# Gate sums begun by ScalarE's zeros, and a new order of products, in a graph layer with a GRU

## The chip, the cores and the metric

The kernel runs on one core of one Trainium2 chip. The metric is the time on the device in microseconds, the median of several runs. Engines are named as in the profile: PE is TensorE's matrix multiply, PEld its weight load, DVE is VectorE, ACT is ScalarE, POOL is GpSimd, SP is SyncE. Everything is computed in float32.

## The reference

There are 64 graphs of 256 nodes with 256 features, and one 256 x 256 adjacency matrix for each. Cut to what matters:

```python
h = relu(layernorm(x))                                   # (64, 256, 256)
c = relu(bn1(conv1d(h.T, conv1_w, 1 tap)))
x_conv = relu(bn2(conv1d(c, conv2_w, 17 taps)) + h.T).T
s = h @ w_se.T + b_se                                    # 3 columns
A = exp(-squared_distance(s, s)) * adj
x_nmp = A @ relu(h @ w_msg.T + b_msg)
gi = concat([x_conv, x_nmp]) @ w_ih.T + b_ih             # r, z, n
gh = h @ w_hh.T + b_hh                                   # r, z, n
r = sigmoid(gi_r + gh_r); z = sigmoid(gi_z + gh_z)
n = tanh(gi_n + r * gh_n)
out = x + (1 - z) * n + z * h
```

## The kernel before

**Tiling.** Two graphs make a pair `i` (512 columns, since nodes lie on the free axis and 128 features on the partitions), and four pairs make a block `b`. There are 32 pairs in 8 blocks. The loop over blocks is unrolled, and what it emits for one block is one long list in which pairs of this block and preparations of the next (`nxt = i + 4`) are woven by hand. Every engine works through its own instructions in the order in which they were emitted; SP and POOL issue the DMAs likewise.

**A block.** The 17-tap convolution is done for the whole block in a transformed domain. `forward` puts the FFT steps `odd` and `even` for VectorE in a queue, `products(b, 0)` to `products(b, 7)` multiply by the transformed filters (line 767, filters `wb` by DMA), and `branch_back`, `odd_back`, `q_back`, `p_back` and `join` bring the result back into `Yv`. `residual` (line 800) adds the input, and a Relu on ScalarE follows (line 801). Each pair also needs `message` (line 804: four groups of products, additions on VectorE at line 813, and the small tile `z`, lines 816 to 822, on ScalarE), `embed` (line 827: three transposes of `z` and a copy to `zT`, line 831), `affinity` (line 834: four small products at line 841, `exp` at line 842, a multiplication by the adjacency on VectorE at line 848) and `aggregate` (line 863, into `xnm`). `conv1` (line 688) is the one-tap convolution for a pair of the next block; `split_steps` are the first FFT steps on its result. `finish` (line 1107) transposes the output, adds `x`, stores it from POOL's queue and loads the next `y` there.

**Gates.** The first pair of each block gets its gate r from ordinary products on 512 columns (`gates_first`). The other gates, n and z of each pair and r of pairs 1 to 3, are 11 in a block and 88 in all. They use a scheme with seven products for a 2 x 2 split (features by graphs): `combine` builds differences of the inputs on VectorE (lines 906 and 911), `weight_sums` those of the weights, and class `Gate` (line 925) makes the seven products, numbered 1 to 7. A gate has two PSUM banks. Products 1 and 2 share one half of the first bank, 7 and 4 the other; 5 has a half of the second, 6 and 3 share the last. Each product is two (gate n) or three (r, z) full products on 256 columns, which follow each other in the sum. Between them the running sum is copied by ScalarE from half 1 into half 6 (line 949), and from half 6 into half 7 (line 952). Sums are finished in `c11`, `c12`, `c22` and `c21`, with additions on VectorE (lines 984, 998, 1014) and tanh on ScalarE (lines 969, 1021). `gate_hn` (line 1030) and `times_r` (line 1036) make r * gh_n. The order of a pair is `gates_r`, then `gates_nz`, to which the loop hands functions (`between`, `middle`, `last`) with the work to be put in between.

**PSUM.** There are eight banks: a ring of three `aux` and a ring of five `acc` (lines 535 and 538). In the kernel before, a product that begins a half carries the start flag, and a product of zeros on the other half of the bank follows it (line 945).

**Pacing.** The order on VectorE is planned while the program is built: class `Pace` keeps a planned time for TensorE and VectorE, and `pace.vector(n, ready, slack)` first emits as many queued FFT steps as fit before the next operation is `ready`. `pace.flush(mark)` emits all up to a mark. `BULK` is a queue of ScalarE copies (adjacency and inputs, lines 435, 660 and 684), of which each product of a gate emits one.

Of the kernel before, what the change touches and what calls it, by code (L numbers as in the profile page):

```python
# [15 lines left out]
BF = mybir.dt.bfloat16  # L16
# [289 lines left out]
def kernel(  # L306
# [145 lines left out]
    zero = const.tile([1, N], BF, name="zero")  # L452
# [87 lines left out]

    PSUM, ACT = 0.2, 0.9
# [146 lines left out]
    def conv1(i):  # L688
        if i >= B // G:
            return  # L690
        for o in range(DC):
            p = acc()
# [9 lines left out]
        pace.vector(0, pace.pe + ACT)  # L702
# [95 lines left out]
    def residual(i, o):  # L798
        v = xcv(i % PB, o)
        nc.vector.scalar_tensor_tensor(v, v, s2[:, o:o + 1], HT[i][:, o, :], op0=ALU.mult, op1=ALU.add)  # L800
        nc.scalar.activation(v, v, AF.Relu, bias=h2_shift[:, o:o + 1])  # L801


    def message(i):
        MSG[i] = work.tile([P, G, MC, D + SE], FP, name="msg")
        for g in range(G):
            for c in range(MC):
                p = acc() if g * MC + c == 3 else aux()
                for k in range(DC):
                    mm(p[:, :D + SE], chunk(HT[i][:, k], g, c), w_msg[:, k, :], D + SE,  # L810
                       start=(k == 0), stop=(k == DC - 1))
                pace.vector(D, pace.pe + PSUM)
                nc.vector.tensor_add(MSG[i][:, g, c, :], p[:, :D + SE], b_msg)  # L813
# [20 lines left out]
    def affinity(i, early=False):  # L834
        E[i] = work.tile([P, G, MC, N], FP, name="e")
        for g in range(G):
            for c in range(MC):
                q = g * MC + c
                p = acc() if q == 3 and not early else aux()
# [43 lines left out]
    def combine(i, q):  # L883
# [7 lines left out]
        def first():  # L891
# [14 lines left out]
            nc.vector.tensor_sub(TERMS[i, q][0], b(0, 1), b(0, 0))  # L906

# [11 lines left out]
    SOON = -0.4  # L919
# [4 lines left out]

    class Gate:
        def __init__(self, i, gate):
            self.i, self.gate, self.bank = i, gate, [acc(), acc()]

        def half(self, j, other=False):
            n, h = WHERE[j]  # L930
            return graph(self.bank[n], 1 - h if other else h)

        def products(self, *js):
            for j in js:
                out = self.half(j)
                qs = (1, 2) if self.gate == N_ else (0, 1, 2)
                for q in qs:
# [3 lines left out]
                    mm(out, weight(q, self.gate, j), v, N, start=(j in (1, 5) and q == qs[0]), stop=(q == qs[-1]),  # L941
                       skip_group_check=True)
                if j in (1, 5):

                    nc.tensor.matmul(self.half(j, True), zero[:, :P], zero, start=False, stop=True,  # L945
                                     skip_group_check=True)
                    pace.tensor(N / 4)
                if j == 5:
                    nc.scalar.copy(self.half(6), self.half(1))  # L949
# [7 lines left out]
                elif j == 7:  # L957
                    self.c22(out)
                elif j == 4:
                    self.c21(out)  # L960
                if BULK:
                    BULK.popleft()()
# [67 lines left out]
    def gate_hn(i, o):  # L1030
        p = acc()
# [7 lines left out]
    def gates_first(i, early, wait):  # L1039

        p = []
        for o in range(DC):
            gate_hn(i, o)
# [6 lines left out]
        for o in range(DC):  # L1050
            product(p[o], i, (2,), o * P, first=False)
        for steps in zip(*(combine(i, q) for q in (1, 2, 0))):
            run(steps)
        for o in range(DC):
            nc.scalar.activation(tr[:, o], p[o], AF.Tanh, bias=b_rz[:, o:o + 1], scale=0.5)
            times_r(o)

    def gates_r(i, between):
        r = Sigmoid(i, R)
        r.products(1, 5, 2, 6)  # L1060
        between()
        gate_hn(i, 0)
        r.products(3, 7)
        gate_hn(i, 1)
        times_r(0)
        r.products(4)
        times_r(1)

    def gates_nz(i, between, middle, last):
        n = New(i, N_)  # L1070
        if i % PB:
            n.products(1, 5)
            z = Sigmoid(i, Z_)
            z.products(1)
            between()
            n.products(2, 6)
            z.products(5)
# [3 lines left out]
        else:  # L1081
            n.products(1)
            z = Sigmoid(i, Z_)
# [11 lines left out]
        last()  # L1095
# [5 lines left out]
        for o in range(DC):  # L1101
# [3 lines left out]
            nc.vector.scalar_tensor_tensor(d[:, o], d[:, o], 0.5, nn[:, o], op0=ALU.mult, op1=ALU.add)  # L1105

# [114 lines left out]
    message(0)  # L1221
    pace.flush(odd)
    run(fft.sums(V, Sv, 0, 0))
    for b in range(NB):
        i = b * PB
        nxt = i + PB
        if b > 0:
            affinity(i)
            load_adj(i + 1)
# [4 lines left out]
        if b > 0:  # L1234
            finish(i - 1)
        else:
            embed(i)
        products(b, 1)
        pace.add(fft.branch_back(Yv, T, 0))
        if b == 0:  # L1240
            affinity(i)
# [18 lines left out]
        message(i + 1)  # L1260
# [19 lines left out]
        def combine_last(j):  # L1280
            pace.flush(joined[j])
            run(combine(i + j, 2))
# [15 lines left out]
        def wait():  # L1298
            pace.flush(scaled)
            affinity(i + 2, True)  # L1300
            conv1(nxt)
# [3 lines left out]
        gates_first(i, lambda i=i: embed(i + 2), wait)  # L1305
# [23 lines left out]
        gates_nz(i, between, lambda: None, last)  # L1329
# [5 lines left out]
        gates_r(i + 1, lambda: BULK.extend(join_h(nxt + 2)))  # L1335
# [21 lines left out]
        gates_nz(i + 1, between, middle, last)  # L1357
        now(join_h(nxt + 3))
        message(i + 3)
        pace.flush(halved)  # L1360
        conv1(nxt + 3)
# [3 lines left out]
        gates_r(i + 2, lambda: embed(i + 3))  # L1365
        pace.flush(normed[0])
        affinity(i + 3)
# [15 lines left out]
        gates_nz(i + 2, lambda: None, middle, last)  # L1383
# [4 lines left out]
        gates_r(i + 3, lambda: None)  # L1388
        bulk()

        def last():
            finish(i + 2)
            if b + 1 < NB:
                message(nxt)
        gates_nz(i + 3, lambda: None, lambda: None, last)
        for n, kind in KINDS[6:]:
            load_kind(b + 1, n, kind)
        if b + 1 < NB:
            pace.flush(odd)
            embed(nxt)  # L1400
            run(fft.sums(V, Sv, 0, 0))
# [46 lines left out]
```

## Time and profile before

| | |
|---|---|
| median of 8 runs | 1913.52 us (1910.41 to 1916.63) |
| profiled execution | 1916.63 us, of which the span of instructions is 1913.5 us |
| granted TensorE clock, mean | 0.983 of full speed |
| busy: PE / PEld / DVE / ACT / POOL | 95% / 73% / 82% / 44% / 13% |
| instructions in the span | 26247 |
| steady period of a block | 223.5 us (from 342.9 to 566.4 us) |

A busy share is the share of the span in which an engine had an instruction in work. The records of matrix products overlap, since products are pipelined and their ends are modelled, so that what a product costs is read from the distance between starts. Weight loads run beside products. In lists of groups the last columns are the idle time of the engine just before these instructions and what ended it. Full products in float32 appear as two records each.

### The profile page before, as it was taken

The page shows a single profiled execution, that of the slowest core. Times are in us where ns is not written, and L with a number is a line of the kernel's source. Part 1 is how long each engine was busy: PE and PEld are TensorE (multiplying, and loading weights), DVE is VectorE, ACT ScalarE, POOL GpSimd, SP SyncE. Part 2 cuts the span into 40 slices and gives each one's busy share as a digit, 9 for nine tenths or more (in the row PEclk, how much of TensorE's full clock was granted, in tenths as well). Part 3 has the DMA queues.
Part 4 walks back from the last instruction along what each step waited for, and adds up shares of the span by engine and source line. Part 5 has one row for each costly group of instructions (what it writes and reads, how often), then busy time and mean ns, then how long its engine had stood idle before and what let it go on. Part 6 is the DMA issues. An engine that isn't in the chain of part 4 may idle for free.

```text
span 1913.5 us, 26247 instructions
## 1 busy us (share of the span) xinstructions
PE 1809.2 (95%) x9062; PEld 1392.0 (73%) x9062; DVE 1575.8 (82%) x3242; ACT 850.4 (44%) x1899; POOL 245.7 (13%) x378
## 2 busy tenths in 40 slices
PE   5999999999999999999999999999999999999996
PEld 3686667867779677886678677796778866786774
DVE  4869878997889878998789987898788986899642
ACT  2534553256432664246532564326542465324431
POOL 3214110200011001110102010110011101010001
PEclk9999999999999999999999999999999999999998
DMA  7775434834447344544448344483445544172001
GB/s 202 244 226 167 105 88 121 236 94 109 97 126 232 86 109 118 165 136 114 96 112 237 99 101 98 123 246 78 110 107 148 170 105 108 52 224 80 23 10 46
DMA packets 250519, 246.23 MB, mean 129 GB/s; under 512 B 143080, under 2 KB 176644, under 8 KB 250387
## 3 DMA queue, kind: packets, MB, share of 16 engines
q1 hardware_dynamic: 216362, 183.31, 34.8%
q0 software_dynamic: 31072, 58.60, 12.6%
q10 hardware_dynamic: 2953, 2.66, 0.7%
q8 instruction: 71, 1.16, 0.3%
q14 instruction: 61, 0.50, 0.1%
HBM read 156.56 MB, written 44.30 MB: 105 GB/s over the span
## 4 chain that ended last, share of the span: by engine, by line
PE 62%; DVE 28%; issue 4%; ACT 3%; DMA 2%; POOL 1%; ACTq 0%; DVEq 0%; POOLq 0%
PE acc L528 52%; PE aux L528 6%; DVE U L60 2%; DVE T L66 2%; DVE U L63 2%; PE aux L532 2%; DVE Yv L63 2%; DVE Yv L66 2%; PE acc L945 2%; DVE V L66 1%; DVE Yv L60 1%; DVE wb L911 1%; DVE msg L813 1%; DVE Yv L800 1%; PE aux L841 1%
## 5 line engine op out<-in xcount | busy, mean ns | idle before, releaser
L528 PE MATMUL acc<-hT,w_hh 128*128 128x512 f32 (+1 forms) x544 | 220.3, 515 | 14.7 <-ACT acc L949 14.7
L528 PE MATMUL acc<-wb,w_s 128*128 128x256 f32 x640 | 165.4, 383 | 0.0
L528 PE MATMUL acc<-wb,w_ih 128*128 128x256 f32 x608 | 160.2, 386 | 4.1 <-DVE Sv L998 4.1
L528 PEld LDWEIGHTS acc<-hT,w_hh 128*128 128x128 f32 x544 | 97.5, 190 | 77.4 <-issue 47.4
L528 PE MATMUL acc<-xnm,w_ih 128*128 128x256 f32 (+1 forms) x416 | 139.4, 423 | 0.0
L528 PE MATMUL acc<-Yv,w_ih 128*128 128x256 f32 (+1 forms) x416 | 135.5, 417 | 1.2 <-ACT Yv L801 1.2
L528 PE MATMUL acc<-V,wb 128*128 128x128 f32 x1024 | 130.7, 282 | 3.8 <-DMA wb<-filt 2.7
L528 PEld LDWEIGHTS acc<-wb,w_s 128*128 128x128 f32 x640 | 121.0, 191 | 18.0
L576 POOL TENSOR_TENSOR rstd<-rstd,neg_half 128x4 f32<-128x4 f32 x32 | 42.3, 1321 | 701.1 <-DVE shift L578 663.3
L998 DVE SCALAR_TENSOR_TENSOR Sv<-Sv,acc 128x256 f32<-128x256 f32 x128 | 53.7, 420 | 93.1 <-PE acc L528 93.0
L528 PEld LDWEIGHTS acc<-wb,w_ih 128*128 128x128 f32 x608 | 112.2, 190 | 24.8 <-DVE Sv L998 7.3
L528 PEld LDWEIGHTS acc<-V,wb 128*128 128x128 f32 x1024 | 125.0, 199 | 4.6 <-issue 2.1
L528 PE MATMUL acc<-U,wb 128*128 128x128 f32 x1024 | 126.1, 278 | 0.2 <-DVE V L783 0.2
L984 DVE TENSOR_TENSOR Sv<-acc,Sv 128x256 f32<-128x256 f32 x112 | 47.4, 423 | 95.6 <-PE acc L528 87.3
L528 PEld LDWEIGHTS acc<-U,wb 128*128 128x128 f32 x1024 | 121.9, 194 | 3.9 <-DVE T L60 1.7
L60 DVE SCALAR_TENSOR_TENSOR V<-T,V 128x256 f32<-128x256 f32 (+2 forms) x224 | 123.3, 609 | 0.3
L528 PE MATMUL acc<-hT,w_c 128*128 128x512 f32 x256 | 121.0, 617 | 2.1 <-ACT hT L644 1.9
L1115 POOL DMA_DIRECT2D out_dram<-y x64 | 39.1, 616 | 593.1 <-DVE y L1114 579.5
L774 ACT COPY d<-acc 128x512 f32<-128x512 f32 x56 | 32.8, 586 | 171.0 <-PE acc L528 65.9
L528 PE MATMUL acc<-xnm,w_s 128*128 128x256 f32 x352 | 107.2, 386 | 0.0
L528 PE MATMUL aux<-e,msg 128*128 128x256 f32 x464 | 104.9, 379 | 0.0
L528 PE MATMUL acc<-Yv,w_s 128*128 128x256 f32 x352 | 104.7, 379 | 0.0
(209 smaller groups left out, 3968.1 us busy)
## 6 DMA issues: line engine op xcount, KB each, us to landing
wb<-filt SPq DMA_DIRECT2D x376, 256.0 KB
y<-in_x_dram POOLq DMA_DIRECT2D x64, 256.0 KB, 5.4
out_dram<-y POOLq DMA_DIRECT2D x64, 256.0 KB, 5.3
x<-in_x_dram SPq DMA_DIRECT2D x60, 256.0 KB
halves_d<-halves SPq DMA_DIRECT2D x116, 128.0 KB
adjh<-halves_d POOLq DMA_DIRECT2D x116, 128.0 KB, 5.0
hh<-halves SPq DMA_DIRECT2D x108, 128.0 KB
filt<-fo POOLq DMA_DIRECT2D x18, 252.0 KB, 5.3
```

The source lines that it names most:

```text
L60: return self.step(out, lambda: self.v.scalar_tensor_tensor(out, x, s, y, op0=ALU.mult, op1=ALU.add))
L63: return self.step(out, lambda: self.v.tensor_add(out, x, y))
L66: return self.step(out, lambda: self.v.tensor_sub(out, x, y))
L528: nc.tensor.matmul(p, w, v, **kw)
L532: nc.tensor.transpose(p, v, ident)
L576: nc.gpsimd.tensor_tensor(t["rstd"], t["rstd"], neg_half, ALU.pow)
L774: nc.scalar.copy(p1, p[0])
L800: nc.vector.scalar_tensor_tensor(v, v, s2[:, o:o + 1], HT[i][:, o, :], op0=ALU.mult, op1=ALU.add)
L945: nc.tensor.matmul(self.half(j, True), zero[:, :P], zero, start=False, stop=True, skip_group_check=True)
L984: nc.vector.tensor_add(v, p, self.sum)
L998: nc.vector.scalar_tensor_tensor(v, v, 0.5, p, op0=ALU.mult, op1=ALU.add)
L1115: nc.gpsimd.dma_start(out=rows(out, G * i + g), in_=row_tile(Y[i], g))
```

## The change

- `Gate.__init__` lets ScalarE copy zeros into halves 1 and 5, the first halves of the gate's two banks, when the banks are taken. The products of zeros and the start flags of the gates are gone; all products of a gate add. `zero` is now one float32 column, read with stride zero.
- The copy from half 1 into half 6 is emitted after product 1 and no longer after product 5.
- All banks of the `acc` ring have been written over their full width by ordinary products before the first gate of each block (one `gate_hn`, two of `p`, two of `conv1`). In the last block, which has no `conv1` there, two full products with the identity are put in their place. Other uses of the ring during the gates move to `aux` (`gate_hn` in `gates_r`, `conv1`, the fourth chunk of `message` and of `affinity`).
- `gates_r` has the order 5, 1, hn, 2, 6, then 5 and 1 of gate n, then 3, 7, hn, 4. Gates are created earlier: n inside `gates_r`, r before other work, in one case inside `last`.
- At the boundary of blocks, `message`, `finish`, `embed`, `affinity` and `load_adj` change places.
- In `wait()`, `conv1` moves between the third and the fourth product of `affinity`.
- Relus after `residual` go through a queue, `RELU`, which products of gates and `relus()` empty. `SOON`, `TIME` and `free` change planned times of `Pace`.

The core of the diff:

```diff
-    zero = const.tile([1, N], BF, name="zero")
+    zero = const.tile([P, 1], FP, name="zero")
...
-    def conv1(i):
+    def conv1(i, pool=None):
...
-            p = acc()
+            p = (pool or aux)()
...
-        pace.vector(0, pace.pe + ACT)
+        pace.vector(0, pace.pe + ACT, SOON)
...
-        nc.scalar.activation(v, v, AF.Relu, bias=h2_shift[:, o:o + 1])
+        RELU.append(lambda: nc.scalar.activation(v, v, AF.Relu, bias=h2_shift[:, o:o + 1]))
...
-                p = acc() if g * MC + c == 3 else aux()
+                p = (last or aux)() if g * MC + c == 3 else aux()
...
-    def affinity(i, early=False):
+    def affinity(i, early=False, between=None):
...
+                if q == 3 and between:
+                    between()
...
             nc.vector.tensor_sub(TERMS[i, q][0], b(0, 1), b(0, 0))
+            TIME[i] = pace.dve + 0.2
...
     class Gate:
         def __init__(self, i, gate):
-            self.i, self.gate, self.bank = i, gate, [acc(), acc()]
+            self.i, self.gate, self.bank = i, gate, []
+            for j in (1, 5):
+                self.bank.append(acc())
+                nc.scalar.copy(self.half(j), zero.to_broadcast([P, N]))
...
             for j in js:
+                if j == 4:
+                    pace.pe = max(pace.pe, self.free)
+                elif j == 5 and pace.pe < TIME.get(self.i, 0):
+                    pace.pe = TIME[self.i]
...
-                    mm(out, weight(q, self.gate, j), v, N, start=(j in (1, 5) and q == qs[0]), stop=(q == qs[-1]),
-                       skip_group_check=True)
-                if j in (1, 5):
-
-                    nc.tensor.matmul(self.half(j, True), zero[:, :P], zero, start=False, stop=True,
-                                     skip_group_check=True)
-                    pace.tensor(N / 4)
-                if j == 5:
-                    nc.scalar.copy(self.half(6), self.half(1))
+                    mm(out, weight(q, self.gate, j), v, N, start=False, stop=(q == qs[-1]), skip_group_check=True)
+                if j == 1:
+                    nc.scalar.copy(self.half(6), out)
+                elif j == 5:
                     self.m5(out)
...
-                if BULK:
-                    BULK.popleft()()
+                for q in (RELU, BULK):
+                    if q:
+                        q.popleft()()
+                        break
...
-            gate_hn(i, o)
+            gate_hn(i, o, acc if o == 0 else aux)
...
             product(p[o], i, (2,), o * P, first=False)
+            nc.scalar.activation(tr[:, o], p[o], AF.Tanh, bias=b_rz[:, o:o + 1], scale=0.5)
+            if o == 0:
+                n = New(i, N_)
...
-    def gates_r(i, between):
-        r = Sigmoid(i, R)
-        r.products(1, 5, 2, 6)
+        n.products(1)
+        return n
+
+    def gates_r(r, between):
+        i = r.i
+        r.products(5, 1)
+        n = New(i, N_)
         between()
         gate_hn(i, 0)
+        r.products(2, 6)
+        n.products(5, 1)
         r.products(3, 7)
+        times_r(0)
         gate_hn(i, 1)
-        times_r(0)
         r.products(4)
         times_r(1)
-
-    def gates_nz(i, between, middle, last):
-        n = New(i, N_)
+        return n
+
+    def gates_nz(n, between, middle, last):
+        i = n.i
+        z = Sigmoid(i, Z_)
         if i % PB:
-            n.products(1, 5)
-            z = Sigmoid(i, Z_)
-            z.products(1)
+            n.products(2, 6)
             between()
-            n.products(2, 6)
-            z.products(5)
+            z.products(5, 1)
             n.products(3, 7)
...
         else:
-            n.products(1)
-            z = Sigmoid(i, Z_)
             z.products(1)
...
-        last()
+        following = last()
...
+        return following
...
-    message(0)
-    pace.flush(odd)
-    run(fft.sums(V, Sv, 0, 0))
     for b in range(NB):
         i = b * PB
         nxt = i + PB
+        pace.flush(odd)
+        run(fft.sums(V, Sv, 0, 0))
+        message(i, acc)
         if b > 0:
-            affinity(i)
-            load_adj(i + 1)
+            finish(i - 1)
...
         products(b, 0)
-        if b > 0:
-            finish(i - 1)
-        else:
-            embed(i)
+        embed(i)
         products(b, 1)
         pace.add(fft.branch_back(Yv, T, 0))
-        if b == 0:
-            affinity(i)
+        affinity(i)
+        if b > 0:
+            load_adj(i + 1)
         products(b, 2)
...
-        message(i + 1)
+        message(i + 1, acc)
...
         def combine_last(j):
             pace.flush(joined[j])
+            relus()
...
         def wait():
             pace.flush(scaled)
-            affinity(i + 2, True)
-            conv1(nxt)
+
+            def between():
+                if nxt < B // G:
+                    conv1(nxt, acc)
+                else:
+                    for _ in range(DC):
+                        nc.tensor.matmul(acc(), ident, HT[i][:, 0, :], start=True, stop=True)
+            affinity(i + 2, True, between)
             pace.add(split_steps(nxt), halved)
             join(2)
             pace.flush(joined[0])
+            relus()
...
-        gates_nz(i, between, lambda: None, last)
+        gates_nz(n, between, lambda: None, last)
+        r = Sigmoid(i + 1, R)
         aggregate(i + 2)
...
         message(i + 3)
         pace.flush(halved)
+        r = Sigmoid(i + 2, R)
         conv1(nxt + 3)
...
-        affinity(i + 3)
+        affinity(i + 3, True)
...
         def last():
             finish(i + 1)
             combine_last(3)
-        gates_nz(i + 2, lambda: None, middle, last)
+            return Sigmoid(i + 3, R)
+        r = gates_nz(n, lambda: None, middle, last)
...
-        def last():
-            finish(i + 2)
-            if b + 1 < NB:
-                message(nxt)
-        gates_nz(i + 3, lambda: None, lambda: None, last)
+        gates_nz(n, lambda i=i: finish(i + 2), lambda: None, lambda: None)
...
-        if b + 1 < NB:
-            pace.flush(odd)
-            embed(nxt)
-            run(fft.sums(V, Sv, 0, 0))
     finish(B // G - 1)
```

## The prediction

> **What bounds the kernel now.** Read first the busy times and the chain of waits of the page.
>
> ```profile
> PE 1809.2 (95%) x9062; PEld 1392.0 (73%) x9062; DVE 1575.8 (82%) x3242; ACT 850.4 (44%) x1899; POOL 245.7 (13%) x378
> PE 62%; DVE 28%; issue 4%; ACT 3%; DMA 2%; POOL 1%; ACTq 0%; DVEq 0%; POOLq 0%
> ```
>
> TensorE is busy 95% and leads the chain; VectorE, with 82%, is the only other engine that can bind. ScalarE has half of its time free. So the question is how much TensorE time the change removes, and whether VectorE lets the kernel have it.
>
> Second, the answer on the tile `zero`, and the TensorE timeline of one gate (a product on 256 columns is two records; columns: start, length).
>
> ```profile
> L945 PE MATMUL acc<-zero x176: 277/278/278, 199.0 to 1883.2; 1*128 1x256 bf16 x176
> ```
>
> ```profile
> 493.48 0.59 PE L528 MATMUL acc<-Yv,w_ih 128*128 128x256 f32 x2
> 494.01 0.28 PE L945 MATMUL acc<-zero 1*128 1x256 bf16 x1
> 494.22 1.56 PE L528 MATMUL acc<-wb,w_s 128*128 128x256 f32 x6
> 495.71 0.28 PE L945 MATMUL acc<-zero 1*128 1x256 bf16 x1
> 496.49 0.70 PE L528 MATMUL acc<-hT,w_hh 128*128 128x256 f32 x2 [0.50 <-ACT acc L949]
> ```
>
> Records overlap, so only starts count. A record of 256 columns is followed by the next after 0.216 us (0.59 for two is two starts and a tail). The pair at 493.48 would be followed at 493.91; the zero product starts 0.10 later, and the next real product 0.21 after that. Over all 176 the medians are 0.096 and 0.208: **one zero product costs 0.304 us of TensorE's time**, not its 0.278 record. After the second one TensorE waits another 0.5 for the copy of line 949.
>
> Third, TensorE's waits (total us, times, longest), and one block boundary in the timeline.
>
> ```profile
> PE acc L528 <- ACT acc L949: 14.7, 24, 3.6
> PE aux L841 <- ACT zT L831: 12.5, 8, 2.5
> PE acc L528 <- DVE Sv L63: 7.3, 7, 1.1
> PE aux L841 <- ACT e L842: 4.3, 8, 1.1
> ```
>
> ```profile
> 563.96 1.03 PE L532 MATMUL aux<-ident,z 128*128 128x128 f32 x3
> 566.42 0.49 PE L841 MATMUL aux<-zT 9*128 9x256 f32 x3 [1.43 <-ACT zT L831]
> 568.24 2.08 PE L528 MATMUL acc<-Sv,wb 128*128 128x128 f32 x8 [1.10 <-DVE Sv L63]
> ```
>
> The block repeats every 223.5 us, with the same waits each time. By starts, a boundary loses 0.28 + 1.65 + 1.47 = 3.4 us (transposes of z, zT, Sv), and each of three gates r loses 0.5 to 0.6.
>
> Fourth, the stretches of one block (length, TensorE, weight loads, VectorE, ScalarE busy).
>
> ```profile
> 500.00:564.00 64.00, 63.55 (x283) 48.77 (x281) 52.21 (x99) 24.71 (x55) 3.62 (x6) 1.00 0.40 100
> 564.00:645.30 81.30, 76.91 (x513) 64.70 (x513) 77.99 (x161) 35.80 (x94) 9.99 (x16) 0.98 0.62 179
> ```
>
> From a boundary to the residuals of the next block (564 to 645), VectorE is busy 78.0 of 81.3 us: there it is nearly the bound. Before it, from 500, it has 12 us free.
>
> [...] the copy of line 949 shows 357, which I use. [...] (line 949 waited 126 us in all for the zero products while copies stood behind it).
>
> **Part by part**, for 8 blocks with 11 gates each, 88 gates.
>
> *Zero products gone:* 176 x 0.304 = **53.5 us**, all on the full engine.
>
> *Copy of half 1 into half 6 after product 1, with other products before 2:* in `gates_r`, `gate_hn` (four records of 512 columns, 4 x 0.43 = 1.7 us) now follows 5 and 1, against about 0.5 us of ScalarE. The 24 waits, 15.9 us by starts beyond the 0.208 counted above (the page's 14.7 allows for the modelled end), go: **15.9**.
>
> *Boundary:* `message` moves behind product 4 of z, `finish` behind it, `embed` behind the first 5.4 us of filter products, `affinity` behind the next. z and zT then have 5 us of cover: 7 x 3.4 = **23.8 us** of waits go. Late next: `finish` takes aux banks that `message`'s additions free on VectorE behind the four d operations (4 x 0.6), sums and residual FFT steps; message covers 16 x 0.218 = 3.5 us. Charge 7 x 0.6 = 4.2. With `finish` two output and two y DMAs move ahead on POOL, and four adjh DMAs move from the boundary to some 16 us later; joined some 31 us after it, they need about 7.5 (2.4 issuing, 5 landing). POOL is 13% busy: nothing; without that margin ScalarE's copies would block. SP's issues keep their order.
>
> *`conv1` inside the affinity in `wait()`:* 3.4 us of products cover the wait for the aux bank: 8 x 0.83 = **6.6**. In `affinity(i + 3, True)` the fourth bank is now an aux bank with no cover: the same 8 x 0.83 = 6.6 come back.
>
> *New waits:* for pair 3, `message` and `finish` no longer stand between products 7 and 4 of z, which share a half; product 4 waits for c22's read, as the profile shows elsewhere (0.74): 8 x 0.74 = 5.9. In pair 0, z's zeros are issued behind n's copy, which waits for n's product 1, and z's product 1 follows at once: 0.1 + 0.36 + 0.36 = 0.8; 8 x 0.8 = 6.4.
>
> *Zero copies:* 176 x 0.36 = 63 us on ScalarE, 850 to 913 busy. The profile doesn't show a stride-zero source: 0.29 to 0.46 us each, from the shorter and longer ACT rows. Elsewhere cover exists: two zeros and a preceding tanh (0.47 + 0.72 = 1.2 us) stand against n's products 2 and 6 (8 x 0.216 = 1.7 us), or against `aggregate` (16 x 0.216 = 3.5). I take nothing there; a bulk copy of 0.77 in between would uncover some 0.3 for a third of the gates, 9 us, which goes to the range. A gain is excluded, as the first product waited for nothing in most gates.
>
> *The five full products* are two of p, one hn and two of conv1, all existing; only in the last block two products (1.7 us) are new, beside a wait of 1.5 us there: 0.2, nothing. hn and conv1 move to three aux banks: their evictions (0.69 and 0.78) fit the 1.7 us of products between; nothing, at most 0.5 a block.
>
> *Pacing and delayed Relus (`SOON`, `TIME`, `free`, `RELU`)* only order existing VectorE and ScalarE work: zero, between -1 and +1 us a block; the wait of 0.68 before n's product 4 in pair 0 stays.
>
> *VectorE:* the stretch before the boundary shortens by about 7 us (message 3.5, twelve zeros 3.65, waits 1.0, new ones off), its VectorE work by 1.4. Of 12 free us some 6 remain, while FFT steps of 0.7 to 1.2 us must fit gaps between gate sums. If half of the lost room can't be made good, 2 to 3 us of steps slide over the boundary. Behind it VectorE has 78.0 + 1.4 and 1 to 2 us of waits on ScalarE, 80 to 82; TensorE has 76.9 + 3.5 and bubbles, 81. The slide is partly absorbed: 7 x 2 = 14 us, between 0 and 6 a block.
>
> Sum: 53.5 + 15.9 + 23.8 + 6.6 = 99.8 less 6.6 + 4.2 + 5.9 + 6.4 + 14 = 37.1, so **62.7 us**. The profiled execution took 1916.6 (span 1913.5 and 3.1 around it): 1854. The median of the runs lies 3.1 lower: **1851**.
>
> **Rivals.** *All is hidden:* VectorE's 14 and half of the other new waits vanish: 99.8 - 11.5 = 88, 1825. For it: free time before the boundary. Against: 96% VectorE behind it.
>
> *VectorE binds behind the boundary:* 6 us a block, 42 in place of 14: gain 35, 1879. The mark would be TensorE waiting for line 63 to 66 results, residuals or messages. For it: the window at 564. Against: TensorE's work in that stretch also grows by message.
>
> *Zero copies become the wait (slower):* if ScalarE starts each gate's pair only when its product is due, behind one bulk copy, each gate pays 0.1 + 0.72 + 0.77 = 1.6: 88 x 1.6 = 140, less the 6.4 counted; gain 62.7 becomes a loss of 71, 1984. It decides from 62.7 / 88 = 0.71 us more per gate. For it: in-order ScalarE, full of waits on products. Against: ScalarE half free, and in the ring of five the bank's last reader is done before, or is ScalarE's own tanh.
>
> [...]
>
> **Numbers.** Forecast 0.52; all hidden 0.18; VectorE binds 0.2; zero copies 0.08; no net change 0.02. The 0.1 for the last two is left out of the range, with parts of the neighbours: 1822 (all hidden, a little beyond) to 1885 (VectorE binds, and the 9 us of uncovered zeros in part). A measurement of this kernel can tell about 0.2%, 4 us: faster 0.9, same 0.02, slower 0.08.
>
> **What would show it.** Right: no record of line 945; 176 ScalarE copies of some 0.36; TensorE's instructions about 172 fewer; no wait for the copy of line 949; no zT wait behind the boundary; the period of a block 215 to 217 us. VectorE's part shows as new waits on Sv, V or msg in the 80 us behind a boundary, and should be near 2 us. Wrong: waits of TensorE on the zero copy over 20 us in all, or a period above 221.

## The result, and the profile after

| | before | after |
|---|---|---|
| median | 1912.15 us (32 runs) | 1895.03 us (11 runs, 1889.77 to 1900.53) |
| ratio after / before | | 0.9909, 95% interval 0.9898 to 0.9920 |
| profiled execution | 1916.63 us | 1894.81 us |
| steady period of a block | 223.4 us | 223.0 us |

The change gains 17 us; 63 were forecast, and 1895 us lies above the forecast range of 1822 to 1885. (The period is the mean of six blocks. The profiled executions differ by 21.8 us; of that, about 3.0 lie before the first residual products, 10.7 in the seven periods that follow, of which 8 in the first, and 6.8 behind the last residual products. The steady block itself gains almost nothing.)

The busy times and the chain of waits of the page after:

```profile
PE 1755.8 (93%) x8890; PEld 1387.8 (73%) x8890; DVE 1580.4 (83%) x3242; ACT 903.1 (48%) x2075; POOL 241.7 (13%) x378
PE 13%; DVE 2%; DMA 1%; ACT 1%; issue 0%; POOL 0%; POOLq 0%; DVEq 0%; ACTq 0%
```

TensorE's busy time did fall by 53 us, and it has 172 instructions fewer. But its share fell from 95% to 93%, so it now waits more. The chain adds up to only 17% of the span: it could be followed back only a short way, and says nothing about the blocks. The waits of TensorE have to be read instead (total us, times, longest):

```profile
PE acc L527 <- ACT Yv L801: 35.2, 8, 5.8
PE acc L527 <- ACT acc L942: 18.7, 22, 3.3
...
PE acc L527 <- DMA wb<-filt: 15.0, 17, 2.5
PE acc L527 <- ACT acc L962: 10.0, 8, 1.3
PE acc L527 <- DVE Sv L1001: 5.7, 10, 0.6
```

Of the waits shown of before, the copy (old line 949), zT and the sums of line 63 are gone. New are the Relu behind the residual (line 801), the zeros (line 942), the filters `wb` (2.7 us before), and the copy from half 1 into half 6 at its new place (line 962). A count of 8 is once in every block.

The answer on the tile `zero`:

```profile
L942 ACT COPY acc<-zero x176: 354/373/416, 193.3 to 1866.0; 128x256 f32<-128x256 f32 x176
...
  PEld acc L527: 32.7, 35
  PE acc L527: 18.7, 22
```

A zero copy has a median of 373 ns. The last two rows say who waited for it; they overlap, since a weight load and its product wait for the same thing.

The block boundary in TensorE's timeline (start, length) has lost its waits. The only one left before it is an ordinary wait for a gate sum, and message, transposes and filter products follow each other:

```profile
545.26 0.70 PE L527 MATMUL acc<-e,w_hh 128*128 128x256 f32 x2 [0.57 <-DVE Sv L1001]
...
546.66 2.79 PE L527 MATMUL aux<-w_msg,hT 128*128 128x259 f32 x12
549.29 1.04 PE L527 MATMUL acc<-w_msg,hT 128*128 128x259 f32 x4
550.18 1.09 PE L531 MATMUL aux<-ident,d 128*128 128x128 f32 x8
551.11 1.06 PE L527 MATMUL acc<-Sv,wb 128*128 128x128 f32 x8
```

The time comes back 80 us later. The chain into the first residual product of a block, in all engines:

```profile
406.06 0.69 PE L849 MATMUL aux<-zT 9*128 9x256 f32 x2
...
409.85 1.42 DVE L800 SCALAR_TENSOR_TENSOR Yv<-Yv,bn_scale,hT 128x512 f32<-128x512 f32 x2
410.70 1.33 ACT L801 ACTIVATE Yv<-Yv,bn_shift 128x512 f32<-128x512 f32 x2 [3.48 <-DVE Yv L800]
...
411.48 2.07 PE L527 MATMUL acc<-Yv,w_ih 128*128 128x512 f32 x2 [4.72 <-ACT Yv L801]
```

TensorE is done with the affinity at 406.8 and stands still until VectorE has made the residual and ScalarE its Relu. From the last start of the affinity to the first residual product it is 5.09 us in six of the blocks, 6.17 in the last one and 1.50 in the first. In before, the product ahead of the residual products is another, and the distance is 0.43 us in all blocks but the last, where it is 1.53.

The wait isn't the whole loss. Behind it the first products on 512 columns start 0.85 us apart in place of 0.43, and in this place the trace has the granted clock at half for 3.4 or 6.8 us (0.50 from 411.1 to 414.4). From the first of these eight products to the start of the ninth it is 5.0 to 6.6 us in the seven blocks with the long wait, against 3.54 in the first block, 13.6 us more in all. In before it is 3.43 us in seven blocks, and 4.97 in the last. The page's row of these products in the after has a mean of 450 ns, in before 417:

```profile
L527 PE MATMUL acc<-Yv,w_ih 128*128 128x256 f32 (+1 forms) x416 | 147.9, 450 | 35.2 <-ACT Yv L801 35.2
```

That the long wait brings the half clock on is the author's reading of its place; no run shows it by itself. Short stretches at half clock stand elsewhere too, also in before: 3.4 us at its last residual products, and 0.50 from 567.9 to 571.2, behind the waits of a boundary.

Why VectorE is late is seen on VectorE itself, one block on. First before, then after, each from the last addition of `message(i + 2)` to the residual:

```profile
630.29 0.42 DVE L813 TENSOR_TENSOR msg<-acc,b_msg 128x259 f32<-128x259 f32 x1
643.09 1.41 DVE L800 SCALAR_TENSOR_TENSOR Yv<-Yv,bn_scale,hT 128x512 f32<-128x512 f32 x2
```

```profile
613.31 0.43 DVE L819 TENSOR_TENSOR msg<-aux,b_msg 128x259 f32<-128x259 f32 x1 [0.45 <-PE aux L527]
614.18 0.43 DVE L819 TENSOR_TENSOR msg<-aux,b_msg 128x259 f32<-128x259 f32 x1 [0.45 <-PE aux L527]
615.06 0.43 DVE L819 TENSOR_TENSOR msg<-aux,b_msg 128x259 f32<-128x259 f32 x1 [0.45 <-PE aux L527]
615.40 1.22 DVE L65 TENSOR_TENSOR Yv<-T 128x1024 f32<-128x1024 f32 x1
...
633.64 1.41 DVE L800 SCALAR_TENSOR_TENSOR Yv<-Yv,bn_scale,hT 128x512 f32<-128x512 f32 x2
```

Before, 12.8 us lie between them, after 18.6. In after VectorE also sits idle between the additions, waiting for TensorE, while the steps that it could do in that time stand behind them in its queue. What it does from there to the residual is FFT steps.

The stretches of a block after (length, then busy time of PE, PEld, DVE, ACT, POOL, the granted clock, DMA share and GB/s): from the residual to the boundary in two parts, and from the boundary to the next residual.

```profile
411.50:475.00 63.50, 60.77 (x242) 45.61 (x243) 52.03 (x121) 38.93 (x77) 5.38 (x8) 0.98 0.39 92
475.00:546.00 71.00, 68.65 (x302) 54.04 (x301) 59.93 (x116) 35.19 (x84) 8.93 (x14) 1.00 0.45 119
546.00:635.30 89.30, 81.67 (x534) 68.48 (x532) 83.20 (x167) 37.46 (x98) 11.30 (x18) 0.97 0.62 169
```

VectorE leaves 11 us in each of the first two stretches unused, and has only 6 free in the third, where TensorE is idle for 7.6.

### The profile page after: what moved, and what is told of

Read it like the earlier page. It is cut to its first block, busy times and chain, and to the rows that moved or that the text cites. A ratio compares the mean times of both kernels' runs of the same rounds, so it can differ in the third digit from the quotient of the medians.

```text
span 1893.0 us, 26098 instructions
## 1 busy us (share of the span) xinstructions
PE 1755.8 (93%) x8890; PEld 1387.8 (73%) x8890; DVE 1580.4 (83%) x3242; ACT 903.1 (48%) x2075; POOL 241.7 (13%) x378
## 5 line engine op out<-in xcount | busy, mean ns | idle before, releaser
L527 PE MATMUL acc<-Yv,w_ih 128*128 128x256 f32 (+1 forms) x416 | 147.9, 450 | 35.2 <-ACT Yv L801 35.2
L527 PE MATMUL acc<-xnm,w_ih 128*128 128x256 f32 (+1 forms) x416 | 135.6, 414 | 0.0
L527 PEld LDWEIGHTS acc<-Yv,w_ih 128*128 128x128 f32 x416 | 83.8, 204 | 66.9 <-ACT Yv L801 42.4
L527 PE MATMUL acc<-hT,w_hh 128*128 128x256 f32 (+1 forms) x320 | 115.6, 455 | 16.6 <-ACT acc L962 10.0
L527 PE MATMUL aux<-w_msg,hT 128*128 128x259 f32 x448 | 105.1, 385 | 5.5 <-DVE msg L819 5.5
L527 PE MATMUL aux<-hT,w_hh 128*128 128x512 f32 x224 | 105.3, 592 | 0.0
L420 POOL DMA_DIRECT2D adjh<-halves_d x116 | 69.1, 614 | 248.7 <-ACT adj L434 187.2
```

Of the source, the lines that this page charges most:

```text
L420: eng.dma_start(out=ADJH[i][:, q], in_=ADJD[i][:, q])
L527: nc.tensor.matmul(p, w, v, **kw)
```

## The experiments

Three theories were to be told apart. **Order on VectorE:** the planner now puts FFT steps, which used to run between gate sums, behind the boundary; TensorE waits for them at the residual. **Throughput of VectorE:** VectorE simply has too much work once TensorE is faster, wherever it stands. **Filters:** the filters `wb` come late, because TensorE asks for them sooner. Beside these, ScalarE's order was suspected for the waits of lines 942 and 962. Gains between different kernels are taken from their ratios to the before, times 1912 us.

**e1: before without the products of zeros.** Their planned time (`pace.tensor(N / 4)`) stays in the program, so the planner orders VectorE's work as in before.

```diff
-                    nc.tensor.matmul(self.half(j, True), zero[:, :P], zero, start=False, stop=True,
-                                     skip_group_check=True)
```

> The kernel before without its 176 products of zeros, all else in place ([...] the sums of the gates are left wrong; the work is otherwise the same). If TensorE alone set the time, 176 x 0.304 = 53.5 us go: 1913 to about 1859. If VectorE's chain from the FFT steps to the residuals of the next block sets the period of seven of the eight blocks, only the parts outside that chain gain: some 15 to 30 us, 1884 to 1898, and TensorE's waits on residuals (line 801), Sv or V appear instead.

Measured: 1870.75 us, ratio 0.9779 (0.9762 to 0.9795), a gain of 42 us, more than the whole change. TensorE's waits in it:

```profile
PE acc L528 <- ACT acc L947: 17.8, 24, 4.4
...
PE acc L528 <- DVE Sv L996: 13.5, 8, 1.9
```

The products were on the path: 42 of the 53.5 us arrive, and 11 don't; longer are the waits for gate sums (13.5; the same line had 4.1 before) and for the copy (17.8; 14.7 before). No steady block waits for the residual. So a faster TensorE with the old plan doesn't bring the wait of line 801; something else in the change does.

**e2 to e4: after with half of each filter loaded, without the adjacency product on VectorE, and with both.**

```diff
-            nc.sync.dma_start(out=WB[b, n, kind], in_=filt[m][:, 3 * (n - PASSES[m][0]) + kind])
+            nc.sync.dma_start(out=WB[b, n, kind][:, 0], in_=filt[m][:, 3 * (n - PASSES[m][0]) + kind, 0])
...
-                nc.vector.tensor_mul(e, e, ADJ[i][:, g * MC + c].rearrange("p (b h c) -> p c h b", c=MC, b=NW))
```

> The changed kernel with half of each transformed filter loaded and used twice (half of the filters is left out). Filter theory: TensorE's 15.0 us of waits for wb go, and VectorE's idle 3.5 us a block before the evictions of the fourth filter product with them, so that the wait of line 801 falls from 5.1 to some 1.5 to 2.5 us a block: 7 x 3.5 = 25 us, 1895 to 1870. VectorE theory alone, filters beside the point: the wait for wb goes, but line 801 takes it over: at most 5 us gained.

> The changed kernel without the multiplication by the adjacency (16 VectorE instructions of 0.53 us a block left out, the order of all others kept). Two of the four groups, 4.2 us, lie between the boundary and the residuals. VectorE theory: line 801's wait of 5.1 us falls by about 4 us a block: 7 x 4 = 28 us, 1895 to 1867. Filter theory: VectorE would only idle longer before the fourth filter product, so half of it, some 12 to 15 us. ScalarE theory (waits on zero copies hold the time): under 5 us.

> Both of the last two edits (half filters, no multiplication by the adjacency). If filters and VectorE together hold line 801's wait, it is gone and the gains add up to 7 x (5.1 + 2) = 50 us, 1845. If one of them alone is the cause, no more than the better of the two.

Measured: e2 1880.24 us, ratio 0.9833 (0.9819 to 0.9848), 15 us under the after; e3 1886.56, 0.9861 (0.9841 to 0.9881), 9 under it; e4 1863.27, 0.9742 (0.9728 to 0.9757), 32 under it. The waits for `wb` are gone in e2. The wait of line 801 is 35.3, 33.2 and 33.2 us in the three, and the distance of starts there stays at 5.09 us in every steady block. For e3:

```profile
PE acc L527 <- ACT Yv L801: 33.2, 8, 4.7
```

Without the adjacency product VectorE has eight instructions fewer between the boundary and the residual, 0.5 us each by starts, and the residual is no earlier against TensorE. That speaks against throughput: VectorE is brought into step with TensorE at the additions of `message(i + 2)`, and from there it needs the same 18.6 us, whatever it had to do before. Filters, too, leave that wait as it is. Why e2 and e3 gain all the same, and together with 32 us more than the sum of both, is not settled by these runs; e12 takes up the filters.

**e5: after with the planned time of TensorE moved on by 6 us in the middle of the filter products**, so that more FFT steps are emitted there.

```diff
+        pace.pe += 6
         products(b, 3)
```

> The changed kernel with one line more, pace.pe += 6 before products(b, 3): no instruction more or less, but the plan emits more queued FFT steps before the evictions of the fourth filter product, so that 11 instead of 19 us of them stand behind the last addition of message(i + 2) (as in the kernel before). Order theory (VectorE is not short of time; steps stand behind additions that wait for TensorE): line 801's wait of 5.1 us a block goes, 25 to 33 us, 1895 to about 1866. VectorE-throughput theory: the same work is late elsewhere (evictions of lines 783 and 784, z), gain under 10 us.

Measured: 1891.70 us, ratio 0.9898 (0.9882 to 0.9915), not told apart from the after by these intervals.

```profile
PE aux L531 <- ACT z L823: 15.9, 7, 2.4
...
PE acc L527 <- ACT Yv L801: 9.0, 8, 1.1
...
PE acc L527 <- DVE V L783: 8.7, 5, 2.0
```

The wait of line 801 falls from 35.2 to 9.0 us, so it is set by where the steps are emitted. But as many steps still stand between boundary and residual, and the wait moves to what VectorE now does later there: `z`, which ScalarE makes from the sums of `message` (15.9), and line 783 (8.7). So VectorE has no room to spare in this stretch, and moving steps within it, as here, doesn't help; e9 lets them leave it.

**e6: after with the ScalarE queue in another order** (z's zeros directly behind product 4 of r, and in pair 0 ahead of product 1 of n; r's zeros at the start of `last` of pair 0; the copy of product 5 behind that of half 1 into half 6).

```diff
+            self.seeded, self.five = False, None
...
                 if j == 1:
                     nc.scalar.copy(self.half(6), out)
+                    self.seeded = True
+                    if self.five is not None:
+                        self.m5(self.five)
                 elif j == 5:
-                    self.m5(out)
+                    if self.seeded:
+                        self.m5(out)
+                    else:
+                        self.five = out
...
+        n.z = Sigmoid(i, Z_)
...
-        z = Sigmoid(i, Z_)
+        z = n.z
...
+            r = Sigmoid(i + 1, R)
```

> The changed kernel with four moves on ScalarE's queue: z of pair 0 is created before n's product 1, z of the other pairs directly after r's product 4, r of pair 1 first in last(), and for the order 5, 1 the copy of sum 5 is emitted after the copy of half 1 into half 6. VectorE's order stays word for word. Order theory (VectorE's chain starts from the messages, so what TensorE saves before is kept): the waits of lines 942 and 962, 18.7 + 10.0 us, go, save some 4 us in the first and last block: 1895 to about 1870. VectorE-throughput theory: line 801's wait grows in return, gain under 12 us.

Measured: 1882.26 us, ratio 0.9846 (0.9827 to 0.9866), 12 under the after.

```profile
PE acc L527 <- ACT Yv L801: 35.2, 8, 5.8
...
PE acc L527 <- ACT acc L943: 4.6, 8, 3.3
```

The zeros' waits fall from 18.7 to 4.6 us and those of the copy from 10.0 to nothing, at the same number of products and copies. TensorE is idle for 16 us less in the profiled execution, but the same products are busy for 4.5 us more (1760.3 us), at a granted clock of 0.973 to 0.977 in the four runs against 0.976 to 0.983 in the after; why the clock is lower stays open. In the timeline of the after one sees how they came about. For r of pair 3:

```profile
519.40 0.68 DVE L1124 SCALAR_TENSOR_TENSOR d<-Sv,d 128x512 f32<-128x512 f32 x1
...
520.17 0.37 ACT L990 COPY Sv<-acc 128x256 f32<-128x256 f32 x1 [3.75 <-DVE d L1124]
520.44 0.77 ACT L434 COPY adj<-adjh 128x512 uint16<-128x512 uint16 x1
521.07 0.41 ACT L962 COPY acc<-acc 128x256 f32<-128x256 f32 x1
...
521.54 0.70 PE L527 MATMUL acc<-hT,w_hh 128*128 128x256 f32 x2 [1.32 <-ACT acc L962]
```

With the order 5, 1 the copy of product 5 (line 990) comes first. It writes a tile that VectorE still reads for the pair before (line 1124), so ScalarE stands for 3.75 us, a bulk copy follows, and only then the copy that product 6 needs. ScalarE lets nothing pass: all 2075 of its instructions in this trace start in the order in which the kernel emits them. The same happens to zeros behind a Relu that waits for VectorE:

```profile
440.12 0.72 ACT L801 ACTIVATE Yv<-Yv,bn_shift 128x512 f32<-128x512 f32 x1 [1.45 <-DVE Yv L800]
440.75 0.66 ACT L942 COPY acc<-zero 128x256 f32<-128x256 f32 x2
441.47 1.56 PE L527 MATMUL acc<-wb,w_s 128*128 128x256 f32 x6 [0.97 <-ACT acc L942]
```

**e7: e5 and e6 together.**

> Both of the last two edits. Order theory: they add up, 50 to 58 us, 1895 to about 1841, below the 1871 of the kernel before without zero products. VectorE-throughput theory: no more than 15 us together.

Measured: 1878.92 us, ratio 0.9832 (0.9805 to 0.9858). Its waits are those of e5 (`z` 16.6, line 801 9.0) without those of line 962. The gain of 15 on the after is that of e6 and about 3 more, within the intervals.

**e8: after with the order of the old boundary** (`message` in `last` of pair 3, then `embed`; `affinity` and `load_adj` at the head of the block; `finish` behind `products(b, 0)`).

```diff
         products(b, 0)
-        embed(i)
+        if b > 0:
+            finish(i - 1)
...
+        def last():
+            finish(i + 2)
+            if b + 1 < NB:
+                message(nxt, acc)
```

> The changed kernel with the order of the kernel before at the boundary of blocks (message and finish before z's product 4, then embed, affinity, filter products). The boundary's waits of 3.4 us return, 7 x 3.4 = 24 us, and those for wb shrink. In its plan 16.8 instead of 19.4 us of FFT steps stand behind message(i + 2). Order theory: line 801's wait falls by 2.3 us a block (16), and with 10 us less for wb the sum is about zero, 1890 to 1900. If the new boundary is what loses the gain (filters come too late for it), it is faster by over 20 us; if the new boundary brings its 24 us, slower by as much.

Measured: 1899.53 us, ratio 0.9939 (0.9916 to 0.9962), only 6 over the after, with intervals that overlap. zT (10.0 us) and the sums of line 62 (7.7) are waited for again, but the wait of line 801 falls from 35.2 to 19.1: what TensorE loses at the boundary VectorE uses to catch up. In the after, the gain at the boundary was mostly given back at the residual.

**e9: after with 0.2 us more of planned time at products 5 and 2 of the gates of pairs 2 and 3**, so that the planner emits more FFT steps between the gate sums. Not an instruction more or less.

```diff
+                if j in (5, 2) and self.i % PB in (2, 3):
+                    pace.pe += 0.2
```

> The changed kernel with 0.2 us added to TensorE's planned time before products 5 and 2 of the gates of pairs 2 and 3: no instruction more or less, but 6 us more of the queued FFT steps are emitted between those gates, so that 55.5 us of them stand between the boundary and the residuals (as in the kernel before) in place of 61.4. Slide theory: the loss behind the boundary is these 6 us; line 801's wait of 5.1 us goes and nothing takes its place: 7 x 4 to 5 = 28 to 35 us, 1895 to 1860 to 1867. Against it (VectorE has no room between the gates): TensorE waits there for lines 1001 and 1015 or for combine, gain under 10 us.

Measured: **1862.37 us, ratio 0.9747 (0.9732 to 0.9761)**, 31 under the after. First TensorE's waits, then VectorE at the additions of `message(i + 2)`:

```profile
PE acc L527 <- DMA wb<-filt: 15.9, 15, 2.6
...
PE acc L527 <- ACT acc L942: 12.9, 16, 3.3
PE acc L527 <- ACT acc L964: 10.0, 8, 1.3
PE aux L531 <- DVE msg L819: 9.4, 14, 1.1
PE acc L527 <- ACT Yv L801: 9.0, 8, 1.1
```

```profile
607.29 0.43 DVE L819 TENSOR_TENSOR msg<-aux,b_msg 128x259 f32<-128x259 f32 x1
607.64 0.68 DVE L62 TENSOR_TENSOR V<-V 128x512 f32<-128x512 f32 x1
608.24 0.42 DVE L819 TENSOR_TENSOR msg<-aux,b_msg 128x259 f32<-128x259 f32 x1
...
609.24 0.42 DVE L819 TENSOR_TENSOR msg<-aux,b_msg 128x259 f32<-128x259 f32 x1
...
622.03 1.42 DVE L800 SCALAR_TENSOR_TENSOR Yv<-Yv,bn_scale,hT 128x512 f32<-128x512 f32 x2
```

Steps stand between the additions again, none of which waits, and 12.8 us lie between the last and the residual, as before the change. At the boundary a wait of 9.4 us is new: the transposes of `finish` need the PSUM banks that the additions of `message` free.

The products behind the residual run at the pace of before again. The 64 records on 512 columns there have a mean of 605 ns, in after 838, in before 618. The page's busy times, and its row with all products of these tiles:

```profile
PE 1743.9 (94%) x8890; PEld 1382.5 (74%) x8890; DVE 1574.6 (85%) x3242; ACT 901.7 (48%) x2075; POOL 245.8 (13%) x378
L527 PE MATMUL acc<-Yv,w_ih 128*128 128x256 f32 (+1 forms) x416 | 134.4, 414 | 9.0 <-ACT Yv L801 9.0
```

So the gain isn't waits alone. Of the 32.7 us between the spans of the two profiled executions, 20.8 are idle time of TensorE, and 11.9 are busy time of the same 8890 records. The mean granted clock is 0.988 to 0.991 in the four runs of e9 and 0.976 to 0.983 in the eleven of the after. Nothing but the order differs, so the order brings both; whether a lower clock would return if the waits alone were gone is not shown.

The time of the FFT steps by place, in us for one block, is an estimate: the emitted order of each kernel, with the durations of the trace.

```
                           before   after    e5     e9     e8
boundary to residual        55.5    61.4    61.5   55.5   60.2
  of it behind the last
  addition of message(i+2)  11.2    19.4    11.2   11.2   16.8
residual to boundary        56.5    50.4    50.5   56.4   51.7
```

The change had moved 6 us of steps over the boundary; e9 moves them back and is the only one of these to gain much. That settles order against throughput of the whole: the work is the same in after and e9. Behind the boundary VectorE does bind, and the order decides how much work stands there.

**e10: e6 and e9 together. e11: e6 with another way to move steps**, a planned price of `n / 960 + 0.07` instead of `+ 0.1` for a step.

> The same edit on top of the four moves on ScalarE's queue (zeros ahead, sum 5 after half 6). If both losses are apart, 13 us from ScalarE and about 30 from the slide: 1895 to about 1852. If only one time can be had once: 1865 or more.

> The four moves on ScalarE's queue, and the plan's price for each VectorE instruction set from n/960 + 0.1 to n/960 + 0.07 us, the distance of starts that the profile shows (0.335 for 256 columns, 0.60 for 512): 54.2 us of FFT steps stand behind the boundary. Slide theory: near the last one, 1850 to 1865. If the place of single steps matters more than their sum, it departs from it by over 15 us.

Measured: e10 **1853.90 us, ratio 0.9703 (0.9678 to 0.9727)**, the best of all kernels here, 57 under the before on its chip and 39 under the after. The two orders add up nearly in full (12 and 31). Its busy times:

```profile
PE 1747.4 (94%) x8890; PEld 1389.3 (75%) x8890; DVE 1573.0 (85%) x3242; ACT 901.2 (49%) x2075; POOL 245.6 (13%) x378
```

e11 is a miss: 1899.07 us, ratio 0.9937 (0.9924 to 0.9951). It brings the steps between boundary and residual down to 54.2, but waits for gate sums come instead, 16.9 us at its line 1022 and 16.7 at line 1008: the cheaper price puts steps in front of sums that TensorE needs at once. How much leaves the stretch is not enough; the single places count. Which of them cost most stays open.

**e12: e10 with half of each filter loaded** (the edit of e2).

> The kernel of e10 with half of each filter loaded and used twice (half of the filters is left out). If waits for wb (12 to 15 us in the changed kernel) are a loss of their own, it gains 12 to 20 us on e10. If they are covered by VectorE's chain, under 5.

Measured: 1859.29 us, ratio 0.9738 (0.9721 to 0.9755), no gain on e10. The waits for `wb` (16.5 in e10) are gone, and `z` is waited for instead:

```profile
PE aux L531 <- ACT z L823: 16.6, 7, 2.4
```

With VectorE on time, the filters' waits cover another that is as long. So late filters are not a loss of their own in e10. That e2 gained 15 in the after remains open; that with the filters early VectorE has more time to catch up there is only argued.

**e13: e10 with the old boundary** (the edits of e8, and 0.15 in place of 0.2 in e9's edit).

> The kernel of e10 with the order of the kernel before at the boundary of blocks; the added plan time is 0.15 us, and 54.1 us of FFT steps stand behind the boundary (55.5 in e10), so that the slide is undone in both. If the new boundary brings its 3.4 us seven times: 1854 to about 1876. If filters that come too late give it back (wb waits fall from 16 to 5 us): 1862 to 1868. If the boundary is worth nothing: 1854.

Measured: 1874.81 us, ratio 0.9808 (0.9794 to 0.9823), 20 over e10. The waits for zT (10.0 us) and the sums (7.7) are back, and those for `finish` (9.4) and most of those for `wb` (12 of 16.5) are gone. In the profiled executions 11 of the 20 us are idle time of TensorE, the rest is busy time of the same products, at a granted clock of 0.976 to 0.981 against 0.985 to 0.991 in e10. So once the order on VectorE is put right, the new boundary is worth 20 us, clock included; in the after (e8) it was worth 6.

**e14: e10 with each zero copy issued twice.**

```diff
-                nc.scalar.copy(self.half(j), zero.to_broadcast([P, N]))
+                for _ in range(2):
+                    nc.scalar.copy(self.half(j), zero.to_broadcast([P, N]))
```

> The kernel of e10 with each zero copy issued twice, 176 copies of 0.36 us more on ScalarE. If zero copies cost only by their place in the queue: under 8 us more, 1854 to 1862. If ScalarE's time is on the path: up to 63 us more; if half of the gates have no cover, 30.

Measured: 1882.66 us, ratio 0.9851 (0.9834 to 0.9867), 28 over e10, or 0.32 us for each of the 88 gates, where 0.75 us of copies were added. ScalarE, busy 49% of the time in e10, has no room for them in many of the places where they stand: the wait for zeros grows from 4.6 to 17.1 us, that for `exp` from 6.5 to 13.1.

## Why the prediction was right and wrong

The direction was right, and so was what it said of TensorE: it binds, and the change takes work and waits from it. The forecast of 1851 us was 44 too low. e10, which differs from the after in the order of the queues of VectorE and ScalarE alone, reaches 1853.9 and returns 39 of the 46 us of gain that were missing. It is another kernel than the one forecast; that it comes within 3 us of 1851 doesn't make the forecast right.

- **Zero products (53.5 us): right as a price, not as a gain.** 42 arrive in e1. The prediction did not ask what each gate waits for next when its products come closer together.
- **Waits for the copy (15.9): half right.** The 24 waits are gone. But in r of pair 3, product order 5, 1 put the copy behind one that waits for VectorE: 8 new waits of up to 1.3 us, 10.0 in all. "About 0.5 us of ScalarE" counted the copy and not what stands ahead of it in the queue.
- **Boundary (23.8 less 4.2): right in its waits, not in what they were worth in this kernel.** The waits for zT and the sums are gone. In the after no wait for `finish` is seen, and most of the gain was lost at the residual (6 us are left, e8). Only in the order of e10 is the boundary worth 20 (e13), close to the 19.6 forecast. The wait for `finish` is there as it was foreseen, with 9.4 us in place of 4.2, and the clock has a part in the 20, so the closeness is in part luck.
- **conv1 in the affinity, and the new waits: right.** Waits for `exp` come once in a block in after as in before, now in `affinity(i + 3, True)` and no longer in `wait()`. By starts, product 4 of z behind product 7 loses 0.737 us a block (forecast 0.74), `affinity(i + 3, True)` 0.828 (0.83). z of pair 0 loses 0.96 (0.8). What the move in `wait()` gains was not tested by itself.
- **Other zero copies ("I take nothing there"): wrong.** The 373 ns were right (0.36 taken, from the 357 ns of the copy of line 949). The cover was wrong. Lines 942 and 962 cost 28.7 us of waits against 6.4 charged; the order of e6 returns 12 us. The prediction's own limit, "over 20 us in all", was just not reached by line 942 alone (18.7); its other limit, a period above 221 us, was passed (223.0), though mainly for the reason that follows: in e9, with ScalarE's order as in the after, it is 218.2.
- **Pacing (zero, -1 to +1 us a block): this is the step that failed.** "Only order existing VectorE and ScalarE work" is true, and the order is what decides. The plan's TensorE time between gates shrinks, and the planner then emits fewer steps there. e8 tells that 1.2 of the 5.9 us come from the new boundary. What else moved them is argued only: the planned time of the zero products is gone (22 a block at 0.108 us, 2.4 us), and `SOON`, `TIME` and `free` change other planned times; these were not tried one by one. What it costs is shown: 35.2 us of waits at the residual, 1.2 in before, and slower products behind them. With the steps moved back e9 is 31 us faster.
- **VectorE (14 us): the mis-sized term that follows from it.** "2 to 3 us of steps slide over the boundary" was the right place; it was 6 us, and behind the last additions of `message(i + 2)` stood 19.4 us of them in place of 11.2. At the residual alone TensorE waits 35.2 us where 14 were charged for all of it. That the products behind seven of these waits ran more slowly (13.6 us in all) has no term in the prediction. The rival "VectorE binds behind the boundary" had the right mark, residuals, and the right size, a slide of 6 us a block; its forecast of 1879 was the nearest of those given. It had chance 0.2, since the slide was thought to be partly absorbed. e5 agrees that VectorE has no room in this stretch; e9 adds that the steps needn't be there.
- **Filters: absent from the sum.** 15.0 us of waits, 2.7 before. They cost nothing by themselves in e10 (e12).

The single errors (21 us more at line 801, 22 at lines 942 and 962, 12 for filters, 11 of the zero products) sum to 66, more than 44, even without the slower products. Here waits in one place gave an engine that was late elsewhere time to catch up (in e8 line 801's waits fell from 35.2 to 19.1 us), or covered other waits (in e12 16.6 us for `z` took the place of 16.5 for `wb`), so they can't be added up.

## What to carry to other kernels

When work is taken from the engine that binds, in a kernel whose order is planned with times, look at where the plan now puts the other engines' filler work, and count it between the same two marks before and after; the busy share of the whole run, 82% and 83% here, shows nothing of it. Behind a long wait, read the distances of the products as well: here the eight that followed took up to 6.6 us in place of 3.5. A cheap instruction on an engine that is half idle can cost what the instruction ahead of it in the queue waits for: here a copy of 0.41 us, on an engine busy 48%, came behind one that had stood for 3.75 us. So place it by that and not by its length. If a wait can be moved by order alone, as in e5, but the time stays, the work has to leave the stretch.

## What was not expected of the hardware

A copy of zeros with a stride-zero source has a median of 373 ns for 128 x 256, and copies of the same size between PSUM halves a mean of 364 and 359 (lines 962 and 966): the source of one column made it no cheaper here. ScalarE at 49% busy charged 0.32 us a gate for 0.75 us of added copies (e14). And the same work, emitted in another order, differs by 31 us (e9 against the after), 12 of them in the busy time of the same products. Behind each of the seven waits of the after with 5 us and more between starts, products started 0.85 us apart in place of 0.43 for part of the next eight, which took 5.0 to 6.6 us. The distance alone doesn't tell it: with 1.50 us, in the first block of the after, they took 3.54, and with 1.53, in the last block of before, 4.97.
